# Two attention blocks in fp32: sums put between products, a bias made later, loads and statistics moved

## Chip, cores and metric

The kernel runs on one core of a Trainium2 chip. The metric is the device time of one execution in microseconds (us), lower is better. All data is fp32. The engines have short names: PE is the matrix engine (TensorE), DVE the vector engine (VectorE), ACT the scalar engine (ScalarE), POOL is GpSimd, and SP is SyncE, which here only issues transfers.

## What is computed

The input is x of shape (8, 512, 32, 32): eight samples of 512 channels at 1024 positions. Two attention blocks follow each other, each with a residual.

```python
# layer 0: group norm (32 groups), 8 heads of 64 channels
h = group_norm(x);  q, k, v = split(W_qkv h + b)
attn = softmax(q^T k / 8);  x = x + W_proj (v attn^T) + b_proj
# layer 1: one norm over the whole sample, one head of 512 channels
n = (x - mean) * rsqrt(var + eps)
q, k, v = Wq n + bq, Wk n + bk, Wv n + bv
attn = softmax(q^T k / sqrt(512));  x = x + Wo (v attn^T) + bo
```

## The kernel before

**Products.** Dense products are done by a seven-product scheme (Strassen's, in the form with sums S1 to S4 of one operand and T1 to T4 of the other), and many of those seven are split once more in the same manner. So most results are built from products into a bank of PSUM that DVE adds onto a tile in SBUF, or ACT copies there. The sums of operands (S, T) are made ahead by DVE or POOL.

**Order.** PE, ACT and DVE run in an order written out by hand (`tc.manual_schedule`); SP's and POOL's orders are set by a scheduler. Each phase is a Python generator that yields after each product or so, its *step*. `at_steps(steps, hooks)` runs the functions in `hooks[n]` after step n. Moving work to another hook thus moves it on its engine's queue. Each engine takes its queue in order.

**Samples.** For each sample b, `layer0` does the softmax attention of layer 0 in 64 *units* (a group of scores, its exponentials, its values), with extra work hung on units by `at_units`. `middle` then makes, for sample b + 1, layer 0's v, the first pair of q and k, and (after the projection of b) the second pair, "qk13"; `attention1` does layer 1 of sample b. For b = 0 to 6 layer 1's q is made by `make_q_twice`, for b = 7 by another path.

The steps and lines that the change touches (numbers are those of the kernel before):

- `make_twice` (in layer 0 of b = 0): for each part of a weight, `begin` re-loads its rows (L595, tile again_wqk), `sums` makes S1 to S4 on DVE (L520, tile wqk_twice), and the last one stores the result (L611). One of these steps is done every second unit. The same units hold `fold`, three transfers on SP (L1300 to L1302), and `folded`, a DVE sum (L1307), which `sum_couple` on PE (L1315, ps_sum) needs.
- qk13 in `middle`: 14 steps of products (L1027) with copies by ACT (L641), then six line products (L1034); between them DVE adds the tiles c12 and c22 (L664) and takes each line's bank (L661). `norm.moments` (L333) makes two passes of ACT over a 128x512 quarter of x for layer 1's statistics; there are eight of them.
- `make_q_twice` with `seven_by_two_steps`: groups z and w, then (second phase) groups c and d. c's products (L1697) go into tiles c by ACT (L703) or DVE (L705); d's are all added onto z (L705). Between the phases DVE puts the bias on z and w (L712). At the end `plus` on DVE adds half of c onto z (L710), for k = 1 and then 0, and POOL adds w to c (L735), which tells the last quarters of q. Here z, c and w carry names z_q, c_q and w_q.
- `norm.untaken` and `norm.bias` (L391 to L402): small DVE instructions on at most four columns. The result of `bias` is used at the end of layer 1 only.
- x_stat: for b + 2, x is loaded once more and ACT makes its moments (L333) during q's second phase and v.
- v of layer 1 (`make_v_twice`, `by_two_steps`): 14 steps of products (L1055), whose results ACT copies (L641) or DVE adds (L638), then six line steps (L783; A11, S2, S3, each for line 0 and line 1) that DVE takes into c_v (L659) after adding c12 and c22 (L664). A line's next product goes onto the same bank, so it waits for DVE's reading of the one before.
- in these v steps `finish_q(n)` (L1777, tile s_q) makes q's S1 to S4, two DVE instructions each, and `halve_a("S1")` (L520, tile S_twice) four more sums. POOL halves S4 and A22 (L520) afterwards, behind its small statistics (L350 to L356).

Of the kernel before, what the change touches and what calls it, by code (L numbers as in the profile page):

```python
# [65 lines left out]
def two_attention_blocks(  # L66
# [18 lines left out]
    nc = tc.nc  # L85
# [494 lines left out]
    def quarters_of_rows(a, rows_of):  # L580
        return {f"A{i + 1}{j + 1}": rows_of(i, a)[:, j, :] for i in range(2) for j in range(2)}

    def make_twice(name, ns=range(2), rows_of=None, engine=nc.vector):

        pairs, key = TWICE.get(name, PAIRS), f"{name}_twice"
        if key not in stored:
            stored[key] = dram.tile([P, len(pairs) * N], FP, tag=key, name=f"stored_{key}")

        def rows_again(n):
            parts, t = {}, tile2(f"again_{name}_{n}")
            for i, (a, _) in enumerate(pairs[n]):
                at = A_PARTS.index(a) * HALF
                nc.sync.dma_start(t[:, i, :], stored[name][:, at : at + HALF])  # L595
                parts[a] = t[:, i, :].rearrange("p (k o) -> p k o", k=2)
            return lambda i, a: parts[a][:, :, i * P : (i + 1) * P]

        def steps_of(n):
            made = []  # L600

            def begin():
                rows = rows_of or rows_again(n)
                made.extend([rows, flat(tile2(f"{name}_twice_{n}"))])

            def sums(i):
                rows, t = made
                sums_a(quarters_of_rows(pairs[n][i][0], rows), t[:, i * HALF : (i + 1) * HALF], engine)
                if i == len(pairs[n]) - 1:
                    size = len(pairs[n]) * HALF  # L610
                    nc.sync.dma_start(stored[key][:, n * N : n * N + size], t[:, :size])  # L611

            return [begin] + [lambda i=i: sums(i) for i in range(len(pairs[n]))]

        return [step for n in ns for step in steps_of(n)]

    def make_all(*args, **more):
        for step in make_twice(*args, **more):
# [60 lines left out]
    def seven_by_two_steps(multiply, at, z, c, w, bias, name):  # L679

        def group(tag, products, use_of):
            line, single = (banks(t, f"ps_{t}{tag}_{name}") for t in "so")
            spares.extend([single[:, 1, :], line[:, 1, :]])  # L690
            line, single = line[:, 0, :], single[:, 0, :]
            for bank, x, y, start, fresh, r, t in [
                (line, "A11", "B11", True, True, 0, 0), (single, "A12", "B21", True, False, 0, 0),
                (line, "S2", "T2", False, True, 0, 1), (single, "S1", "T1", True, True, 1, 1),
                (line, "S3", "T3", False, False, 1, 1), (single, "S4", "B22", False, False, 0, 1),
                (line, "A22", "T4", False, True, 1, 0),
            ]:
                multiply(bank, products, x, y, start)
                tiles, always = use_of
                to = at(tiles, r, t)  # L700
                of = bank[:, : len(products) * 2 * P].rearrange("p (i q) -> p i q", i=to.shape[1])
                if fresh and not always:
                    nc.scalar.copy(to, of)  # L703
                else:
                    nc.vector.tensor_tensor(to, of, to, ALU.add)  # L705
                yield

        def plus(to, x, y, by=None):
            if by is None:
                nc.vector.tensor_tensor(to, x, y, ALU.add)  # L710
            else:
                nc.vector.scalar_tensor_tensor(to, x, by, y, ALU.add, ALU.add)  # L712

        def in_order(order, **groups):
            for n in order:
                next(groups[n])
                yield

        spares.clear()
        first = dict(z=group("z", REST[0], (z, False)), w=group("w", REST[1], (w, False)))  # L720
        yield from in_order("zzwzwzwzwzwzww", **first)
        for k in range(2):
            plus(z[k][:, 1, :], z[k][:, 0, :], z[k][:, 1, :], bias and bias(k, 0))
        for k in range(2):
            plus(w[k], w[k], z[k][:, 1, :], bias and bias(k, 1))
        spares.clear()
        c_of, d_of = [("S1", "T1"), ("A22", "T4")], [("A12", "B21"), ("S4", "B22")]
        second = dict(c=group("c", c_of, (c, False)), d=group("d", d_of, (z, True)))
        yield from in_order("ccdcdcdcdcdcd", **second)
        next(second["d"])  # L730
        for k in [1, 0]:
            plus(z[k][:, 1, :], z[k][:, 1, :], c[k][:, 0, :])
        for k in range(2):
            both = w[k].unsqueeze(1).to_broadcast([P, 2, HALF])
            nc.gpsimd.tensor_tensor(c[k], c[k], both, ALU.add)  # L735
        yield
        spares.clear()

# [407 lines left out]
    def layer0(bs, qs, ks, vs, b, norm_next, ending, begun):  # L1146


        if b == 0:
            vs[:] = places_v(f"0_{b}")  # L1150
            hooks = {}
# [64 lines left out]
        if b == 0:  # L1216
            w = next_weight("qk13")
            w.finish()
            p0 = waiting[-1]

            def bias0():
                rows = Rows([(bias_0, p0.moving)], 1, "bias0", room("bias0"))
                rows.store()
                rows.fetch(nc.sync)
                throughs[:] = [rows]

            hooks = {
                4: [lambda: norm_next.mean_of_all()], 5: [lambda: norm_next.variance_of_all()],
                **{6 + half: [lambda half=half: norm_next.normed(norm_next.xs, [half])] for half in range(2)},
                8: [bias0, lambda: combine.first(norm_next.xs), lambda: score(0)],  # L1230
                9: [combine.second, lambda: score(1), lambda: make_all("qk13", rows_of=both_of(w))],
            }
            hooks[7].append(p0.finish)
            at_steps(together(*pairs_qk(w, 1, bs, qs, ks, b)), hooks)
            steps = []
            for name, ns in [("v0", range(2)), ("p0", range(2)), ("wqk1", range(4))]:
                of = [columns_of(of) for of in waiting if of.name == name]
                steps += make_twice(name, ns, of[0] if of else None)
            for n, step in enumerate(steps):
                at_units.setdefault(3 + 2 * n, []).append(step)  # L1240
        else:
            ps[0], = begun
            accs[units[0][:2]] = ps[0]
            score(1)
            if norm_next is not None:

                def load_next():
                    norm_next.xs = load_x(b + 1, nc.sync)

                at_units[8] = [load_next]  # L1250
                at_units[12] = [norm_next.of_deviation]
                for n in range(2 * NC):
                    at_units[14 + n] = [lambda cc=n % NC, half=n // NC: norm_next.normed_one(norm_next.xs, cc, half)]
                at_units[22] = [lambda: combine.take(norm_next.xs)]
                for n in range(4):
                    at_units[23 + 3 * n] = [lambda n=n: combine.make(n + 1)]
        for n, step in enumerate(ending):
            at_units.setdefault(n + 2, []).append(step)
        last = norm_next is None
# [129 lines left out]
        for i in range(2, len(units) + 2):  # L1389
# [10 lines left out]
            name = f"0_{b}_{pair}_{g}"  # L1400
# [36 lines left out]
        norm = norm1(xs, b)  # L1437
# [50 lines left out]
        hooks = {2: [ready.load]}  # L1488
# [7 lines left out]
    def middle(b, bs, twice_w, twice_b, comb, combine2, bias, hooks_v, divisions):  # L1496
# [15 lines left out]
        hooks = {n: [division] for n, division in enumerate(divisions)}  # L1512
# [16 lines left out]
        pairs = places_qk(1, b + 1)  # L1529
        hooks = {10: [ready.load]}  # L1530
        for n in range(2 * NC):
            hooks.setdefault([2, 4, 6, 8, 10, 12, 14, 14][n], []).append(
                lambda cc=n % NC, half=n // NC: norm.moments(cc, half, half == 0)
            )
        for n in range(1, 5):
# [29 lines left out]
    def attention1(xs, norm, ready, b, at_values, norms):  # L1565

        last = b + 1 == B
# [169 lines left out]
        else:  # L1737
            hooks = {
                0: [norm.both_halves], 6: [lambda: spares.insert(0, spares[3])], 7: [norm.mean_of_all],
                10: [lambda: spares.pop(0)], 11: [norm.deviation],  # L1740
                13: [norm.untaken, lambda: biases.append(norm.bias())],
                16: [lambda: twice_w.append(WeightTwice("wvo1"))],
            }
            if b + 2 < B:
                later = []
# [24 lines left out]
        def finish_q(n):  # L1770
            of[f"S{n}"] = halves(tile2(f"s{n}_q_{b}"))
            x, y, op = {
                1: ("A21", "A22", ALU.add), 2: ("S1", "A11", ALU.subtract),
                3: ("A11", "A21", ALU.subtract), 4: ("A12", "S2", ALU.subtract),
            }[n]
            for k in range(2):
                nc.vector.tensor_tensor(of[f"S{n}"][k], of[x][k], of[y][k], op)  # L1777

        v_pairs = places_v(f"1_{b}")
        for n in range(1, 5):  # L1780
            hooks_v.setdefault(2 * n + (3 if last else 5), []).append(lambda n=n: finish_q(n))
        hooks_v.setdefault(17 if last else 15, []).append(lambda: halve_a("S1"))
        at_steps(make_v_twice(w, twice_w[0], bs, twice_b, v_pairs, f"v_1_{b}"), hooks_v)


# [891 lines left out]
```

## Time and profile before

| | before |
|---|---|
| median of 3 runs | 2799.12 us (2797.68 to 2799.32) |
| profiled execution | 2798.8 us, its span 2797.1 us |
| granted clock of PE | 0.999 |
| PE busy | 2772.4 us, 99% of the span |
| DVE, ACT, POOL busy | 77%, 42%, 21% |
| DMA | 358.59 MB, mean 128 GB/s |

One stretch of b = 0, from the table of busy times by window:

| stretch, us | what runs | length | PE busy | DVE busy | ACT busy | POOL busy |
|---|---|---|---|---|---|---|
| 248.0 to 293.0 | q and k pair 0, projection | 45.00 | 45.00 | 35.89 | 6.17 | 15.77 |
| 293.0 to 316.2 | q and k pair 1 (qk13) | 23.20 | 22.47 | 16.35 | 15.82 | 21.49 |
| 316.2 to 338.4 | layer 1's q | 22.20 | 21.83 | 14.77 | 11.90 | 3.13 |
| 338.4 to 363.1 | layer 1's v | 24.70 | 23.33 | 19.04 | 11.55 | 14.03 |
| 363.1 to 453.0 | scores and values of layer 1 | 89.90 | 89.90 | 69.29 | 23.43 | 25.50 |

The span runs from the program's first to its last instruction; the time of an execution has 1.7 us around it. "Busy" is the time in which an engine has an instruction under way. PE's ends are modelled, and its short stops are partly hidden in the busy time. The list of waits says which engine's idle time ended with which release, as total, times and longest.

### The profile page before, as it was taken

To read this page: it belongs to the slowest core of one execution; us is meant where nothing else is said; L and a number is where in the kernel's file an instruction comes from. 1 tells how busy PE (TensorE), PEld (TensorE's weight loads), DVE (VectorE), ACT (ScalarE), POOL (GpSimd) and SP (SyncE) were. 2 spreads that over 40 slices of the span, in tenths; PEclk is the share of its full clock that TensorE was granted. 3 is DMA by queue.
4 is the path that set the end of the run, shared out by engine and by line. 5 is a ranking of instruction groups with operands and counts; after the bars stand their busy time and mean duration, and the time that the engine had idled before them with its cause. 6 is when DMAs were issued, how large, how long until landed. Compare 5 with 4: busy or idle time off the path is not lost.

```text
span 2797.1 us, 41715 instructions
## 1 busy us (share of the span) xinstructions
PE 2772.4 (99%) x16318; PEld 1645.5 (59%) x16318; DVE 2147.5 (77%) x3023; ACT 1186.7 (42%) x1911; POOL 598.2 (21%) x612
## 2 busy tenths in 40 slices
PE   9999999999999999999999999999999999999999
PEld 5437764377643776447764477645676356753375
DVE  6787677876778777887778776877768877688877
ACT  3462533625346153462535524255342643226621
POOL 0001440014400253003530044300432005320121
PEclk9999999999999999999999999999999999999999
DMA  7545514265142642326432263322633236141101
GB/s 256 204 129 196 202 57 140 58 210 182 57 140 58 211 181 74 126 62 230 155 115 86 77 226 143 127 81 70 240 128 140 69 102 238 69 169 31 35 16 39
DMA packets 114525, 358.59 MB, mean 128 GB/s; under 512 B 25052, under 2 KB 25852, under 8 KB 107920
## 3 DMA queue, kind: packets, MB, share of 16 engines
q1 hardware_dynamic: 89856, 299.68, 31.3%
q10 hardware_dynamic: 24464, 56.16, 6.1%
q8 instruction: 130, 2.13, 0.3%
q14 instruction: 75, 0.61, 0.1%
HBM read 252.77 MB, written 79.21 MB: 119 GB/s over the span
## 4 chain that ended last, share of the span: by engine, by line
PE 91%; DVE 5%; POOL 1%; issue 1%; ACT 1%; DMA 1%; ACTq 0%; SPq 0%; DVEq 0%; POOLq 0%
PE ps_o L1185 15%; PE s L1136 15%; PE ps_o L1995 10%; PE ps_l L1827 5%; PE ps_l_qk L1034 5%; PE ps_s L1810 4%; PE ps_l_v L783 4%; PE ps_s L1827 4%; PE ps_s_qk L1027 3%; PE ps_l_p L768 3%; PE ps_o_qk L1027 2%; PE ps_s_v L1055 2%; PE ps_s_p L1092 2%; PE ps_s_two L2125 2%; PE ps_o_v L1055 2%; PE ps_o_two L2125 1%
## 5 line engine op out<-in xcount | busy, mean ns | idle before, releaser
L940 ACT ACTIVATE p<-s 128x1024 f32<-128x1024 f32 x505 | 516.3, 1024 | 308.5 <-PE s L1136 301.4
L942 DVE TENSOR_TENSOR acc<-acc,p 128x1024 f32<-128x1024 f32 x384 | 468.7, 1221 | 61.8 <-ACT p L940 52.6
L1136 PE MATMUL s<-qk_back,qk_back 64*64 64x512 f32 x3528 | 457.4, 590 | 0.0
L1185 PE MATMUL ps_o<-p,v_back 64*64 64x512 f32 x3528 | 455.3, 589 | 0.0
L1185 PEld LDWEIGHTS ps_o<-p,v_back 64*64 64x64 f32 x3528 | 134.8, 133 | 243.7 <-issue 239.9
L1136 PEld LDWEIGHTS s<-qk_back,qk_back 64*64 64x64 f32 x3528 | 132.5, 133 | 245.6 <-issue 216.2
L537 POOL TENSOR_TENSOR B_twice_p<-o 128x512 f32<-128x512 f32 x14 | 20.9, 1493 | 1067.9 <-DVE o L1205 1067.9
L1995 PE MATMUL ps_o<-t_p,s_v 128*128 128x512 f32 x384 | 169.6, 596 | 0.0
L1801 ACT ACTIVATE p<-p,factor 128x512 f32<-128x512 f32 (+1 forms) x112 | 84.5, 780 | 113.3 <-DVE p L1837 86.4
L1815 ACT COPY p<-ps_s 128x512 f32<-128x512 f32 x96 | 53.1, 588 | 175.9 <-PE ps_s L1810 175.9
L1837 DVE TENSOR_TENSOR p<-ps_l,p 128x512 f32<-128x512 f32 x136 | 91.6, 688 | 44.8 <-PE ps_l L1827 43.2
L1995 PEld LDWEIGHTS ps_o<-t_p,s_v 128*128 128x128 f32 x384 | 71.8, 190 | 88.4 <-issue 88.0
L659 DVE TENSOR_TENSOR c_v<-ps_l_v,c_v 128x512 f32<-128x512 f32 x120 | 79.2, 686 | 44.8 <-PE ps_l_v L783 44.7
L537 POOL TENSOR_TENSOR B_twice<-x 128x512 f32<-128x512 f32 x23 | 35.6, 1550 | 358.6 <-DVE x L1447 177.2
L942 DVE TENSOR_TENSOR acc<-p,p 128x1024 f32<-128x1024 f32 x57 | 69.7, 1222 | 49.1 <-ACT p L940 49.1
L1034 PE MATMUL ps_l_qk<-t,w_qk 128*128 128x512 f32 x224 | 100.3, 595 | 2.3 <-DVE c_k L661 2.1
L1837 DVE TENSOR_TENSOR p<-ps_s,p 128x512 f32<-128x512 f32 x112 | 74.8, 686 | 31.3 <-PE ps_s L1827 29.7
L641 ACT COPY c_q<-ps_s_qk 128x512 f32<-128x512 f32 x56 | 32.6, 583 | 139.4 <-PE ps_s_qk L1027 139.4
L641 ACT COPY c_v<-ps_s_v 128x512 f32<-128x512 f32 x90 | 52.7, 585 | 91.1 <-PE ps_s_v L1055 91.1
L1798 POOL TENSOR_TENSOR acc<-acc,p 128x512 f32<-128x512 f32 x48 | 83.5, 1740 | 13.3 <-ACT p L1801 10.8
L1034 PEld LDWEIGHTS ps_l_qk<-t,w_qk 128*128 128x128 f32 x224 | 42.0, 190 | 58.3 <-issue 50.2
L373 POOL TENSOR_TENSOR rstd<-rstd,minus_half 128x4 f32<-128x4 f32 (+1 forms) x16 | 12.9, 806 | 273.1 <-DVE rstd L372 273.1
(693 smaller groups left out, 5815.4 us busy)
## 6 DMA issues: line engine op xcount, KB each, us to landing
x<-in_x SPq DMA_DIRECT2D x64, 512.0 KB, 9.3
qk_back<-kept_qk SPq DMA_DIRECT2D x56, 512.0 KB, 6.6
w_qk<-stored_qk SPq DMA_DIRECT2D x14, 1792.0 KB
fold<-acc SPq DMA_DIRECT2D x56, 256.0 KB, 2.9
qk_twice<-stored_qk_twice ACTq DMA_DIRECT2D x28, 512.0 KB, 4.8
kept_v<-c_v SPq DMA_DIRECT2D x28, 512.0 KB, 4.4
kept_qk<-c_q SPq DMA_DIRECT2D x28, 512.0 KB, 2.6
kept_qk<-c_k SPq DMA_DIRECT2D x28, 512.0 KB, 3.5
```

The costliest lines, as they stand in the source:

```text
L783: nc.tensor.matmul(bank[:, u * 2 * P : (u + 1) * 2 * P], bs[b][:, k, n * P : (n + 1) * P], w[a][:, k, :], start=fresh and u == k == 0, sto ...
L940: nc.scalar.activation(p, s, AF.Exp, scale=factor)
L942: nc.vector.tensor_tensor(acc, first, p, ALU.add)
L1027: nc.tensor.matmul(bank[:, i * 2 * P : (i + 1) * 2 * P], parts[a][x], twice_b[v][y], start=start and i == 0, stop=True, skip_group_check=True,
L1034: nc.tensor.matmul(bank, of(i, a)[:, k, :], bs[v][:, k, :], start=start and k == 0, stop=k == 1, skip_group_check=True,)
L1055: nc.tensor.matmul(bank[:, (2 * i + u) * P : (2 * i + u + 1) * P], twice_b[v][y][:, u * P : (u + 1) * P], parts[a][x], start=start and i = ...
L1136: nc.tensor.matmul(s[cols, j, :], ks[pair][k0 // HALF][rows, k0 % HALF : k0 % HALF + HD], qs[pair][g][rows, :], start=True, stop=True,)
L1185: nc.tensor.matmul(o[cols, half, :], vs[n][kt % 4 // 2][rows, h, c0 : c0 + HD], p[rows, j, :], start=kt == 0, stop=kt == NT - 1,)
L1810: nc.tensor.matmul(bank, bs[v][:, k, t * P : (t + 1) * P], of[a][k], start=a == "A11" and k == 0, stop=k == 1, skip_group_check=True,)
L1827: nc.tensor.matmul(bank[:, u * 2 * P : (u + 1) * 2 * P], v[y][:, u * P : (u + 1) * P], a[x], start=start and u == 0, stop=True, skip_group ...
L1837: nc.vector.tensor_tensor(at(r, t), bank, at(r, t), ALU.add)
L1995: nc.tensor.matmul(bank, v_parts[kt // 2][a][:, kt % 2, c * P : (c + 1) * P], p_parts[kt // 2][b][:, kt % 2, cols], start=fresh and kt == ...
```

## The change

- `make_twice` gets an argument `early`, set for weights that have to be re-loaded (wqk1): the re-load for the next part then stands in front of the sums of the present one.
- In `seven_by_two_steps` the additions of c onto z, and POOL's of w to c, become `exchange(k)`: k = 0 between d's fifth and sixth product, k = 1 after the seventh. Before, both stood after the seventh, k = 1 first for z.
- In qk13 the moments of step 12 are moved to step 14.
- In layer 1's q for b < 7, `norm.bias` moves from step 13 to step 20.
- In layer 1's v for b < 7, `finish_q(1..4)` move from steps 7, 9, 11, 13 to 5, 7, 9, 11, and `halve_a("S1")` from step 15 to 13.

The order of PE's instructions stays as it was, as does POOL's but for its two additions of w to c; on ACT one copy of c_k changes places with two passes.

```diff
--- before.py
+++ after.py
@@ -580,7 +580,7 @@
     def quarters_of_rows(a, rows_of):
         return {f"A{i + 1}{j + 1}": rows_of(i, a)[:, j, :] for i in range(2) for j in range(2)}
 
-    def make_twice(name, ns=range(2), rows_of=None, engine=nc.vector):
+    def make_twice(name, ns=range(2), rows_of=None, engine=nc.vector, early=False):
 
 
 
@@ -612,7 +612,13 @@
 
             return [begin] + [lambda i=i: sums(i) for i in range(len(pairs[n]))]
 
-        return [step for n in ns for step in steps_of(n)]
+        steps = [steps_of(n) for n in ns]
+        if early:
+            begins = [of.pop(0) for of in steps]
+            for of, begin in zip(steps, begins[1:]):
+                of.insert(0, begin)
+            steps[0].insert(0, begins[0])
+        return [step for of in steps for step in of]
 
     def make_all(*args, **more):
         for step in make_twice(*args, **more):
@@ -726,13 +732,17 @@
         spares.clear()
         c_of, d_of = [("S1", "T1"), ("A22", "T4")], [("A12", "B21"), ("S4", "B22")]
         second = dict(c=group("c", c_of, (c, False)), d=group("d", d_of, (z, True)))
-        yield from in_order("ccdcdcdcdcdcd", **second)
-        next(second["d"])
-        for k in [1, 0]:
+
+        def exchange(k):
             plus(z[k][:, 1, :], z[k][:, 1, :], c[k][:, 0, :])
-        for k in range(2):
             both = w[k].unsqueeze(1).to_broadcast([P, 2, HALF])
             nc.gpsimd.tensor_tensor(c[k], c[k], both, ALU.add)
+
+        yield from in_order("ccdcdcdcdcdc", **second)
+        exchange(0)
+        yield from in_order("d", **second)
+        next(second["d"])
+        exchange(1)
         yield
         spares.clear()
 
@@ -1235,7 +1245,7 @@
             steps = []
             for name, ns in [("v0", range(2)), ("p0", range(2)), ("wqk1", range(4))]:
                 of = [columns_of(of) for of in waiting if of.name == name]
-                steps += make_twice(name, ns, of[0] if of else None)
+                steps += make_twice(name, ns, of[0] if of else None, early=not of)
             for n, step in enumerate(steps):
                 at_units.setdefault(3 + 2 * n, []).append(step)
         else:
@@ -1529,7 +1539,7 @@
         pairs = places_qk(1, b + 1)
         hooks = {10: [ready.load]}
         for n in range(2 * NC):
-            hooks.setdefault([2, 4, 6, 8, 10, 12, 14, 14][n], []).append(
+            hooks.setdefault([2, 4, 6, 8, 10, 14, 14, 14][n], []).append(
                 lambda cc=n % NC, half=n // NC: norm.moments(cc, half, half == 0)
             )
         for n in range(1, 5):
@@ -1738,8 +1748,8 @@
             hooks = {
                 0: [norm.both_halves], 6: [lambda: spares.insert(0, spares[3])], 7: [norm.mean_of_all],
                 10: [lambda: spares.pop(0)], 11: [norm.deviation],
-                13: [norm.untaken, lambda: biases.append(norm.bias())],
-                16: [lambda: twice_w.append(WeightTwice("wvo1"))],
+                13: [norm.untaken], 16: [lambda: twice_w.append(WeightTwice("wvo1"))],
+                20: [lambda: biases.append(norm.bias())],
             }
             if b + 2 < B:
                 later = []
@@ -1778,8 +1788,8 @@
 
         v_pairs = places_v(f"1_{b}")
         for n in range(1, 5):
-            hooks_v.setdefault(2 * n + (3 if last else 5), []).append(lambda n=n: finish_q(n))
-        hooks_v.setdefault(17 if last else 15, []).append(lambda: halve_a("S1"))
+            hooks_v.setdefault(2 * n + 3, []).append(lambda n=n: finish_q(n))
+        hooks_v.setdefault(17 if last else 13, []).append(lambda: halve_a("S1"))
         at_steps(make_v_twice(w, twice_w[0], bs, twice_b, v_pairs, f"v_1_{b}"), hooks_v)
 
 
```

## Prediction

> **What bounds the kernel now.** TensorE (PE) does. Part 1 of the page, the busy table, gives it 99% of the span, and the chain of waits gives it 91% of the path. So only time in which PE stands still can be won, and no edit takes matmuls away.
>
> ```profile
> PE 2772.4 (99%) x16318; PEld 1645.5 (59%) x16318; DVE 2147.5 (77%) x3023; ACT 1186.7 (42%) x1911; POOL 598.2 (21%) x612
> ...
> PE 91%; DVE 5%; POOL 1%; issue 1%; ACT 1%; DMA 1%; ACTq 0%; SPq 0%; DVEq 0%; POOLq 0%
> ```
>
> The busy table hides part of each stop, because a matmul's end is modelled. I therefore read the list of waits first (total, times, longest), to find where PE waits for another engine, and then took start-to-start times from the timeline.
>
> ```profile
> DVE s_q L1777 <- POOL c_q L735: 15.2, 7, 2.2
> ...
> PEld ps_l_v L783 <- DVE c_v L659: 13.6, 14, 1.8
> ...
> PEld ps_l_qk L1034 <- DVE c_k L661: 8.1, 7, 2.2
> ...
> PEld ps_sum L1315 <- DVE acc L1307: 7.1, 7, 2.3
> ...
> PEld ps_oc_q L1697 <- DVE c_q L705: 5.4, 7, 0.8
> ...
> DVE wqk_twice L520 <- DMA again_wqk<-stored_wqk: 4.8, 2, 2.7
> ```
>
> Seven times almost always means once in each of the seven samples whose layer 1 makes q in two phases (b = 0 to 6). The timeline of b = 0 (start, duration, engine, line; idle before it and its releaser in brackets) shows each stop:
>
> ```profile
> 177.85 1.06 PE L1315 MATMUL ps_sum<-acc,ones 64*32 64x512 f32 x8 [1.37 <-DVE acc L1307]
> ...
> 308.32 0.56 ACT L641 COPY c_k<-ps_s_qk 128x512 f32<-128x512 f32 x1
> ...
> 310.91 5.42 PE L1034 MATMUL ps_l_qk<-t,w_qk 128*128 128x512 f32 x12 [0.73 <-DVE c_k L661]
> ...
> 327.06 0.16 DVE L402 TENSOR_TENSOR bias<-v_b,bias 128x4 f32<-128x4 f32 x1
> ...
> 329.79 0.68 DVE L705 TENSOR_TENSOR c_q<-ps_oc_q,c_q 128x512 f32<-128x512 f32 x1
> ...
> 330.53 1.13 PE L1697 MATMUL ps_oc_q<-T_twice,wqk_twice 128*128 128x256 f32 x4 [0.37 <-DVE c_q L705]
> ...
> 345.27 1.29 DVE L1777 TENSOR_TENSOR s_q<-z_q,c_q 128x512 f32<-128x512 f32 x2 [2.18 <-POOL c_q L735]
> ...
> 353.77 0.68 DVE L659 TENSOR_TENSOR c_v<-ps_l_v,c_v 128x512 f32<-128x512 f32 x1
> ...
> 354.52 3.71 PE L783 MATMUL ps_l_v<-w_wvo,t 128*128 128x256 f32 x16
> ...
> 358.00 0.94 DVE L520 TENSOR_TENSOR S_twice<-s_q,S_twice 128x256 f32<-128x256 f32 x1
> ...
> 359.60 3.72 PE L783 MATMUL ps_l_v<-w_wvo,t 128*128 128x256 f32 x16 [1.37 <-DVE c_v L659]
> ```
>
> A 128x256 matmul starts every 0.215 us, a 128x512 one every 0.43. The 16 that start at 354.52 should be followed at 357.97, and are at 359.60: 1.64 us lost, a slow restart of 0.10 included. Counted so over the trace, these stops cost:
>
> - v's lines (L783): 1.64 in b = 0 to 5, 1.38 in b = 6; 11.2 in all.
> - q and k of layer 0, pair 1 (L1034): 1.00 in b = 0, 1.67 in b = 4, 0.31 in the others; 4.2.
> - q's second phase (L1697): 0.64 in each, and in b = 1 a further 1.2; 5.7.
> - the sum in layer 0 of b = 0 (L1315): 1.95, once.
>
> Together 23.0 us, 0.8% of the span: the most that the edits can bring.
>
> [...] S_twice (L520) takes 0.78 to 0.94 us beside POOL at 355 to 359, the same shape (spare, L520) 0.42 alone at 369, and sums from PSUM (L705) stay at 0.69 beside POOL at 341. [...] the three instructions of V's bias, on 1 to 4 columns, take 0.15, 0.23 and 0.16. [...]
>
> **The change, part by part.** The instructions are the same in number and kind, and PE's and POOL's orders are unchanged but for POOL's two additions of w to c, now c[0] first.
>
> *Weights of layer 0, b = 0.* The re-load of each part of wqk1 is put one step, two units of 1.72 us, ahead of its use; SP issues two of its loads ahead of a fold's three. DVE's wait of 2.67 at 171.84 goes, so the fold's sum (L1307, 176.58 to 177.80) comes some 2.7 earlier and PE no longer loses 1.95. The other samples, with no such loads, have no stop there. Gain 1.95 (bounds -2 to 1.95: on SP the fold's three transfers now stand behind the second early load, and if that waits for a free buffer, the fold is late and PE's stop as long as now or twice that).
>
> *The moments moved from step 12 to 14.* ACT, in order, does c_k's copy at 306.38, then two passes (1.94), then c_k's other copy at 308.32, for which DVE and then PE wait. Now the copies are adjacent: the second ends near 307.5, DVE adds the two c_k tiles (0.7, or 1.28 with POOL) and takes the bank from 308.5 to 309.25, before PE's 310.03. The passes end when they did. Gain 4.2 (3 to 4.2).
>
> *V's bias moved to step 20.* Three instructions, 0.52 from 326.62 to 327.14, leave the DVE chain in front of L712 and L705, so PE's next start moves from 330.53 to 330.02. At step 20 DVE stands idle for 0.51 (until ACT's c_q at 333.76): free. But ACT is late next. It starts its passes over x_stat at 329.59, when a load lands, and its copies of c follow behind them, at 331.21 and 333.17; PE must wait for each before it rewrites the bank. In b = 0 the second allows PE's bank at 333.78 instead of 334.09. Doing this sum with each sample's copies leaves 0.22, 0, 0.10, 0.60, 0, 0.21 and 0.60 (b = 6 has no x_stat): 1.7. If the loads land earlier, up to 4.5; if later, 0.
>
> *Additions of C into Z, and the finishing of q.* The first addition goes into DVE's idle 1.03 ahead of 337.75. POOL's first addition can then start near 337.4 rather than 340.17, and the pair (2 x 2.54) ends near 343.4, allowing 0.7 for the second DVE addition[...], instead of 345.24. So finish_q's first sum, two steps earlier, starts at 343.0 to 343.5, and two of its eight instructions more fit before DVE's c_v at 346.86, which waits for ACT. From c_v's second (347.75, set by PE) DVE runs without a gap, a sum every 0.60: 6 to the end of finish_q and c_v, then halve_a's four (0.37 each alone), then c12 and the line's addition. The old order had eight before c12. So the addition starts at 347.75 + 0.61 + 6 x 0.60 + 1.47 + 0.60 = 354.03, and PE may go on at 354.78, when it is due at 354.51: 0.27 lost, 0.37 with the restart. The stop of 1.64 is gone since the four are now in front. Gain 1.27, but POOL's small statistics lie beside the four here; I take 1.15, in six samples 6.9. In b = 6 there are no statistics, and POOL's halving of S4 begins just when DVE's four do: they take 2.93, as at 2411.55, and c12 0.5 more, so the stop grows from 1.38 to some 2.2: minus 0.8. Sum 6.1; bounds -4 (all samples as b = 6, and some more) to 9.
>
> Sum: 1.95 + 4.2 + 1.7 + 6.1 = 13.95, some 14.0. The profiled execution took 2798.8 (span 2797.1, 1.7 around it); less 14.0 is 2784.8. The median of the runs is 0.3 above it: **2785.1**.
>
> **The rivals.**
>
> 1. *The four in front are a new wait.* If halve_a meets POOL in every sample, v's gain is -0.8 x 7 = -5.6 to 0, and the sum 2.3 to 7.9: 2791 to 2797. For it: 0.94 against 0.42 in b = 6. Against: in b = 0 to 5, POOL's S4 waits for statistics that ACT ends at 353.3, and starts at 355.34. Chance 0.12.
> 2. *PE loses nothing more.* The x_stat loads land early and the lines wait for nothing: 2777 to 2780. Against: ACT's copies have 0 to 0.6 us of room. Chance 0.13.
> 3. *Slower: finish_q waits on DVE's queue behind POOL.* Its first two sums (four instructions, 2.4) and one c_v (0.6) come before the c_v that PE allows at 347.75, so all behind is late by POOL's end less 344.75. If POOL gains no head start[...], POOL ends near 346.1 and everything is 1.35 late; with the halving under POOL as well (2.0 more) v's stop is 0.37 + 1.35 + 2.0 = 3.7. The loss is 7 x (3.7 - 1.6) = 14.7 against 7.85 from the other edits: 2806. It is slower by over 0.2% from a stop of 3.5, thus from POOL's end at 345.9, where 345.24 is now. Against: POOL's start moves up by 2.8. Chance 0.04.
> 4. *It does not do what it says*: the stops go but PE waits as long for the next engine. Some 2793.5 to 2799; chance 0.05.
>
> **How the numbers follow.** The forecast has 0.66 and a range of its own of 2781 to 2789, which takes in the bounds of the two smaller open costs (1.7, and 6.1 give or take 3). 0.2% is 5.6 us, about what a measurement of this kernel can tell from no change. Faster by more than that: the forecast, rival 2 and most of rival 1, 0.89. Within: 0.07. Slower: 0.04. The range to hold 8 in 10 takes the forecast with half of rivals 1 and 2: 2778.5 to 2791.
>
> **What would show it.** In the profile after, "PEld ps_l_qk <- DVE c_k" and "DVE wqk_twice <- DMA" should be gone; ps_oc_q's wait for DVE under 1 us in all, with waits for ACT's c_q copies in its place; ps_l_v still waiting for DVE, at S2 of line 0, about 0.3 us in b = 0 to 5 and 1.7 or more in b = 6; POOL's first c_q sum starting some 1.0 us before PE's first v product, where it starts 1.8 after it now. A v stop over 1.5 us in b = 0 to 5, or DVE waiting for POOL's c_q as long as now, would prove the largest term wrong.

## The result, and the profile after

The changed kernel takes 2782.11 us (median of 4 runs, 2781.19 to 2782.54); the kernel before, beside it, 2798.44 (4 runs). The ratio is 0.9941, with a 95% interval of 0.9924 to 0.9958: faster by 16.3 us, 0.6%. The forecast was 2785.1 in a range of 2778.5 to 2791.0. The profiled execution took 2782.46, with a span of 2780.7 (before: 2798.8 and 2797.1), again at a granted TensorE clock of 0.999.

The page of the kernel after, busy table and chain of waits:

```profile
PE 2770.3 (100%) x16318; PEld 1646.2 (59%) x16318; DVE 2139.4 (77%) x3023; ACT 1187.9 (43%) x1911; POOL 590.3 (21%) x612
...
PE 95%; DVE 2%; DMA 1%; ACT 1%; issue 0%; ACTq 0%; SPq 0%; DVEq 0%
```

PE has the same 16318 matmuls and fills the span; its share of the path rose from 91% to 95%, and DVE's fell from 5% to 2%. The list of waits of the kernel after (who waits, for whom: total us, times, longest) shows what replaced the stops:

```profile
PEld ps_l_v L793 <- DVE c_v L665: 5.4, 7, 2.5
...
PEld ps_sc_q L1707 <- ACT c_q L709: 2.7, 4, 1.0
...
PEld ps_oc_q L1707 <- ACT c_q L709: 1.7, 6, 0.3
PEld ps_oc_q L1707 <- DVE c_q L711: 1.7, 7, 0.2
...
PEld ps_l_qk L1044 <- DVE c_k L667: 0.8, 1, 0.8
```

v's wait fell from 13.6 to 5.4, of which 2.5 is one sample; qk's from 8.1 to 0.8; q's for DVE from 5.4 to 1.7, and waits for ACT's copies (2.7 and 1.7) came in its place. DVE's 15.2 for POOL's c_q and its 4.8 for the re-loaded weights are no longer there. The timeline of b = 0 shows v's part (after, lines of DVE, POOL and PEld in order of start):

```profile
334.56 2.36 POOL L739 TENSOR_TENSOR c_q<-c_q,w_q 128x1024 f32<-128x1024 f32 x1 [11.64 <-DVE z_q L716]
337.55 2.36 POOL L739 TENSOR_TENSOR c_q<-c_q,w_q 128x1024 f32<-128x1024 f32 x1 [0.63 <-DVE z_q L716]
340.13 1.28 DVE L1787 TENSOR_TENSOR s_q<-z_q,c_q 128x512 f32<-128x512 f32 x2
...
349.07 0.42 DVE L520 TENSOR_TENSOR S_twice<-s_q 128x256 f32<-128x256 f32 x1
...
350.20 0.42 DVE L520 TENSOR_TENSOR S_twice<-s_q,S_twice 128x256 f32<-128x256 f32 x1
350.54 0.69 DVE L670 TENSOR_TENSOR c_v<-c_v,c_v 128x512 f32<-128x512 f32 x1
351.14 0.68 DVE L665 TENSOR_TENSOR c_v<-ps_l_v,c_v 128x512 f32<-128x512 f32 x1
...
351.88 0.73 PEld L793 LDWEIGHTS ps_l_v<-w_wvo,t 128*128 128x128 f32 x4 [0.48 <-DVE c_v L665]
```

POOL ends its pair at 339.91, before DVE's s_q at 340.13 wants it, and the four halvings run alone at 0.42 us each. PE's next bank starts at 351.88, where 348.18 (start of the 16 matmuls before) plus 3.45 gives 351.64: 0.24 lost. In b = 6 the same code meets POOL:

```profile
2393.52 0.94 DVE L520 TENSOR_TENSOR S_twice<-s_q 128x256 f32<-128x256 f32 x1
...
2394.14 0.91 POOL L520 TENSOR_TENSOR S_twice<-S_twice,s_q 128x256 f32<-128x256 f32 x1
2394.39 0.94 DVE L520 TENSOR_TENSOR S_twice<-s_q,S_twice 128x256 f32<-128x256 f32 x1
...
2395.25 1.20 DVE L670 TENSOR_TENSOR c_v<-c_v,c_v 128x512 f32<-128x512 f32 x1
...
2397.11 5.04 PEld L793 LDWEIGHTS ps_l_v<-w_wvo,t 128*128 128x128 f32 x24 [2.49 <-DVE c_v L665]
```

A halving lasts up to 0.94 in place of 0.42, c12's sum (L670) 1.20 in place of 0.69, and PE stops for 2.25. One kernel thus shows the same DVE instructions with POOL's halving beside them (b = 6, POOL's L520 from 2392.54 on) and without it (b = 0, where POOL's begins at 352.44, behind them).

**A count without thresholds.** PE's order is the same in all these kernels, so each stage can be timed from the start of its first matmul to the start of the next stage's. The table gives, for each kernel, its stage lengths less those of the kernel before, summed over the samples, in us. "Start" is all before the first scores of b = 0 (106.2 us in the kernel before), with the first loads of the weights; in e3 to e5, whose edits lie behind it, it is 0.49 and 0.68 shorter and 0.17 longer. "To q" runs in b = 0 from these scores to the start of layer 1's q, and in the later samples from the end of v to the next q (the stops of ps_sum and ps_l_qk lie there). "All" ends at PE's last matmul.

| kernel | start | to q | q | v | all |
|---|---|---|---|---|---|
| changed | +0.40 | -6.01 | -1.81 | -7.24 | -14.65 |
| e1, re-load alone | -0.48 | -3.15 | -0.67 | 0.01 | -4.26 |
| e2, moments alone | -0.26 | -3.84 | -1.13 | -0.03 | -5.24 |
| e3, bias alone | -0.49 | 0.04 | -2.31 | -0.01 | -2.78 |
| e4, exchange alone | -0.68 | 0.07 | -0.66 | -0.02 | -1.30 |
| e5, finishing and halving alone | +0.17 | -0.36 | +1.74 | -3.48 | -1.91 |
| e6, changed, halving at 15 | +0.34 | -5.54 | -2.20 | -3.32 | -10.73 |
| e7, changed, passes later | +0.56 | -6.05 | -0.88 | -7.49 | -13.86 |
| e8, e6 and e7 | +0.36 | -6.05 | -0.89 | -3.66 | -10.24 |
| e9, changed, halving at 17 | +0.41 | -5.99 | -1.68 | -11.74 | -18.97 |
| e10, changed, passes spread | +0.14 | -5.96 | -4.94 | -7.32 | -18.05 |
| e11, e9 and e10 | +0.15 | -6.07 | -4.94 | -11.74 | -22.60 |
| e12, before, passes spread | -0.23 | 0.16 | -1.19 | -1.05 | -2.30 |

A *late load* means here that x_stat lands late, so that ACT's passes over it, and the copy of c_q behind them, are late and PE waits. The kernel before had one in b = 1 in its profiled execution, worth 0.9 to 1.2. So e1, e2 and e4, whose edits don't touch PE's waits for ACT in q, show that "gain" in q too (in e1 and e4 a late load in b = 0 takes 0.3 and 0.6 of it back), and so does e12. Of the span's 16.3 us, 14.65 are PE's; 1.7 lie between PE's last start and the end of the span, 7.27 before and 5.58 after. DVE's last sum ends 5.9 and 4.2 before the end, and after it only the final write is left. In the profiles of the seven kernels with the change (after, e6 to e11) this tail is 5.58 to 5.79; in the seven without it, it is 5.94 to 6.00 (e4, e5, e12) or 7.25 to 7.44 (before, e1 to e3). So most of the 1.7 varies without the change, and why the tail is shorter in all seven kernels with it was not traced: whether the change has a part in it stays open.

### The profile page after: what moved, and what is told of

Read it like the earlier page. It is cut to its first block, busy times and chain, and to the rows that moved or that the text cites. A ratio compares the mean times of both kernels' runs of the same rounds, so it can differ in the third digit from the quotient of the medians.

```text
span 2780.7 us, 41752 instructions
## 1 busy us (share of the span) xinstructions
PE 2770.3 (100%) x16318; PEld 1646.2 (59%) x16318; DVE 2139.4 (77%) x3023; ACT 1187.9 (43%) x1911; POOL 590.3 (21%) x612
## 4 chain that ended last, share of the span: by engine, by line
PE 95%; DVE 2%; DMA 1%; ACT 1%; issue 0%; ACTq 0%; SPq 0%; DVEq 0%
PE ps_o L1195 16%; PE s L1146 16%; PE ps_o L2005 10%; PE ps_l_qk L1044 5%; PE ps_l L1837 5%; PE ps_l_v L793 5%; PE ps_s L1820 4%; PE ps_s L1837 4%; PE ps_s_qk L1037 3%; PE ps_s_v L1065 3%; PE ps_o_qk L1037 3%; PE ps_l_p L778 3%; PE ps_o_v L1065 2%; PE ps_s_two L2135 2%; PE ps_s_p L1102 2%; PE ps_o_two L2135 1%
## 5 line engine op out<-in xcount | busy, mean ns | idle before, releaser
L667 DVE SCALAR_TENSOR_TENSOR c_q<-ps_l_qk,vec,c_q 128x512 f32<-128x512 f32 x56 | 40.8, 749 | 39.7 <-PE ps_l_qk L1044 39.7
```

## The experiments

In the edits shown below, lines are shortened (`...` for what is left out), and the `.append(...)` behind each `setdefault` is left out.

**e1 to e4: one edit at a time, on the kernel before.**

```diff
e1  -        return [step for n in ns for step in steps_of(n)]
    +        steps = [steps_of(n) for n in ns]
    +        if early:
...
    +                steps += make_twice(name, ns, of[0] if of else None, early=not of)
e2  -  [2, 4, 6, 8, 10, 12, 14, 14][n]
    +  [2, 4, 6, 8, 10, 14, 14, 14][n]
e3  -  13: [norm.untaken, lambda: biases.append(norm.bias())],
    +  13: [norm.untaken], ... 20: [lambda: biases.append(norm.bias())],
e4  +  exchange(k), as in the change, nothing else
```

> The kernel before with one edit alone: the re-load of each part of layer 0's weights in b = 0 one step earlier. Theory (four separate stops of TensorE, each taken away by its own edit): the stop in front of ps_sum in b = 0 goes, and s<-q,k of b = 0 starts some 2.0 us earlier (176.9 for 178.9); every later stage keeps its distance, so the span is 2.0 shorter, 2795. Rival (the stop goes but TensorE waits for the next fold or for the weights instead): 0 to 1 us, with a new wait of ps_sum or of s. Rival (SP's queue late): a longer wait of acc for kept parts, 0 to 2 us slower.

Measured: 2794.95 us, before 2797.96, ratio 0.9988 (0.9981 to 0.9995). Timeline of b = 0, e1; all 16 matmuls of ps_sum now run in one piece, where before (in the prediction's lines) the second eight waited:

```profile
174.95 0.18 PEld L1321 LDWEIGHTS ps_sum<-acc,ones 64*32 64x32 f32 x16 [0.81 <-DVE acc L1313]
174.95 1.09 PE L1321 MATMUL ps_sum<-acc,ones 64*32 64x512 f32 x16
```

The scores behind ps_sum in b = 0 start 2.4 us earlier, counted from the first scores of b = 0, and 0.7 of the stop of ps_l_qk in b = 0 goes as well: 3.1, more than expected. The 0.7 comes from two places that the edit doesn't touch: ACT's gap at its loads of wqk_twice is 1.02 where it was 1.31, and DVE's sum into c_k takes 0.87 where it took 1.28. Why the two changed with the shift in time was not traced.

> The kernel before with one edit alone: the moments of layer 0 measured after step 14 instead of step 12. Theory (separate stops): the stops of ps_l_qk go, 0.3 in five samples, 1.0 in b = 0 and 1.4 in b = 4, as they did with all edits together: 3.9 us, 2794 to 2795. Rival (they go only because other edits move the loads of the statistics in time): under 2 us. The wait of ps_l_qk for c_k should be gone from the list but for one.

Measured: 2794.77, ratio 0.9989 (0.9982 to 0.9996). "To q" falls by 3.84, as expected; ACT's two copies of c_k lie together and PE goes on without a wait in six samples. In b = 4, where the stop was 1.67, 0.3 of it stays. Timeline of b = 0 in e2:

```profile
304.65 3.60 PE L1034 MATMUL ps_l_qk<-x,w_qk 128*128 128x512 f32 x8
306.16 1.05 ACT L641 COPY c_k<-ps_s_qk 128x512 f32<-128x512 f32 x2
308.09 4.45 PE L1034 MATMUL ps_l_qk<-t,w_qk 128*128 128x512 f32 x10
```

> The kernel before with one edit alone: V's bias made after step 20 of q instead of step 13. Theory (separate stops, ScalarE's passes late next): ps_oc_q starts 0.53 us earlier in each of seven samples, and 0 to 0.8 of it is given back in front of ps_sc_q and ps_oc_q, where they wait for ScalarE's copies behind its passes over x_stat; 1.7 to 2.1 us in all, 2796 to 2797. Rival (the copies are late only because all else is earlier): the full 3.5 to 5.

Measured: 2797.03, ratio 0.9995 (0.9986 to 1.0004), which alone tells nothing from no change. In the trace ps_oc_q starts 0.53 us earlier in all seven samples, 3.7 in sum, and waits for ACT's copies take part of it back, in front of ps_sc_q (0.78 late in b = 0) and ps_oc_q: q is 2.31 shorter, of which 0.85 is the late load of b = 1. Timeline of b = 0, e3:

```profile
329.56 1.13 PE L1697 MATMUL ps_oc_q<-T_twice,wqk_twice 128*128 128x256 f32 x4
...
331.52 0.59 ACT L703 COPY c_q<-ps_sc_q 128x512 f32<-128x512 f32 x1
...
332.16 1.13 PE L1697 MATMUL ps_sc_q<-T_twice,wqk_twice 128*128 128x256 f32 x4 [0.61 <-ACT c_q L703]
```

The theory holds, with a gain that depends on when a load lands.

> The kernel before with one edit alone: the additions of C into Z, and GpSimd's two additions after them, put between the last products of q; the finishing of q and the halving of S1 stay where they were. Theory (an order on VectorE's queue, not GpSimd, sets v's stop): VectorE's wait for GpSimd's c_q (15.2 us in the list) goes, and yet v's stops stay at 1.6 us in b = 0 to 5, since the same ten additions and c_v's lie between TensorE's last bank of ps_s_v and its first line: 0 us gained, within 1 us of the kernel before. Rival (VectorE's idle 2.2 us behind GpSimd is what v waits for): the stop falls by more than 1 us per sample, 7 to 9 us gained.

Measured: 2796.68, ratio 0.9996 (0.9987 to 1.0005). v is unchanged to 0.02 us in every sample. DVE's wait for POOL is gone, and DVE stands about as long further on (timeline of b = 0, e4):

```profile
342.97 1.28 DVE L1780 TENSOR_TENSOR s_q<-z_q,c_q 128x512 f32<-128x512 f32 x2
346.81 0.69 DVE L638 TENSOR_TENSOR c_v<-ps_s_v,c_v 128x512 f32<-128x512 f32 x1 [2.56 <-ACT c_v L641]
```

So the wait that heads the prediction's list, 15.2 us, was worth nothing alone: behind it the next instruction of DVE waits for ACT. The rival, 7 to 9 us gained, is out.

**e5: the finishing of q and the halving, without the exchange.**

```diff
-  hooks_v.setdefault(2 * n + (3 if last else 5), [])
-  hooks_v.setdefault(17 if last else 15, [])    # halve_a
+  hooks_v.setdefault(2 * n + 3, [])
+  hooks_v.setdefault(17 if last else 13, [])
```

> The kernel before with the finishing of q two steps earlier and the halving of S1 at step 13 instead of 15, but with the additions of C into Z and GpSimd's two additions left where they were. Theory (the exchange gains nothing alone but is what lets the earlier finishing run): VectorE still waits for GpSimd until 345.2 of b = 0 and two additions more now stand in front of c_v, so everything from c_v on is 0.5 us later than with all edits; v's stop is 0.75 to 0.9 in b = 0 to 5, for 1.64 before and 0.35 with all edits, and some 2.8 in b = 6: 6 x 0.8 - 1.4 = 3 us gained in all (2 to 5). Rival (the exchange isn't needed): the stop is 0.35 as with all edits, 6.7 gained. Rival (c_v's banks, late behind the two additions, stop TensorE at ps_s_v too): 0 gained or slower.

Measured: 2795.30, before 2798.14, ratio 0.9988 (0.9982 to 0.9995). v: -0.82 in b = 0 to 5, +1.47 in b = 6, sum -3.48, expected 3. Timeline of b = 0, e5:

```profile
347.20 1.30 DVE L1777 TENSOR_TENSOR s_q<-z_q,c_q 128x512 f32<-128x512 f32 x2 [2.18 <-POOL c_q L735]
...
353.00 3.62 PE L783 MATMUL ps_l_v<-w_wvo,x 128*128 128x256 f32 x16
...
357.22 0.94 PEld L783 LDWEIGHTS ps_l_v<-w_wvo,t 128*128 128x128 f32 x5 [1.01 <-DVE c_v L659]
```

DVE still stands 2.18 us for POOL, now ahead of more work, and PE's line starts 0.77 late (357.22 less 353.00 and 3.45). In v the exchange alone gives 0, this part alone 3.5, both 7.2: the exchange frees time that only the earlier finishing uses. (q was 1.71 longer in b = 0 here, a late load.)

**e6 to e8: what is left, first attempts, on the changed kernel.**

```diff
e6  -  hooks_v.setdefault(17 if last else 13, [])
    +  hooks_v.setdefault(17 if last else 15, [])
e7  -  hooks.setdefault([14, 17, 19, 21][n], [])      # measure_later
    +  hooks.setdefault([19, 19, 21, 21][n], [])
e8  both
```

> The changed kernel with one thing put back: the halving of S1 at step 15 of v, behind the lines' first two additions, instead of 13. Theory (the earlier finishing and GpSimd's head start are what won, the halving in front is a cost): without its four instructions (1.5 us alone, some 3 beside GpSimd) in front, c12 and the line's first addition come 1.5 earlier and wait for TensorE instead; v's stops of 0.35 in b = 0 to 5 go, and the 2.35 of b = 6 falls to 0.8 or less: 3 to 4 us below the changed kernel, some 2778.5. Rival (the halving ahead of the lines is what took the stop away): v's stops come back to 1.4 to 1.6 in every sample, 7 us above the changed kernel.

Measured: 2786.42, before 2798.14, ratio 0.9958 (0.9944 to 0.9972): 4.3 above the changed kernel's median, where the theory said 3 to 4 below. The stops in front of the second bank went, 0.24 and 2.25, but another came at the third bank (timeline of b = 0, e6):

```profile
352.14 1.59 POOL L520 TENSOR_TENSOR S_twice<-s_q 128x256 f32<-128x256 f32 x2
352.69 0.45 DVE L520 TENSOR_TENSOR S_twice<-s_q 128x256 f32<-128x256 f32 x1
...
354.80 0.94 DVE L520 TENSOR_TENSOR S_twice<-s_q,S_twice 128x256 f32<-128x256 f32 x1
...
355.66 1.28 DVE L665 TENSOR_TENSOR c_v<-ps_l_v,c_v 128x512 f32<-128x512 f32 x2
...
356.40 0.92 PE L793 MATMUL ps_l_v<-w_wvo,t 128*128 128x256 f32 x3 [0.90 <-DVE c_v L665]
```

The halving beside POOL lasts from 352.69 to 355.66 and the addition that frees the bank stands behind it: 1.06 us. So the theory fell, and the changed kernel's place ahead of POOL is part of its gain in b = 0 to 5.

> The changed kernel with ScalarE's first two passes over x_stat put after step 19 of q instead of 14 and 17, that is behind its copies of c from ps_sc_q and ps_oc_q. Theory (what is left of q's stops is ScalarE waiting for a load with those copies behind it): the copies run at 13.2 and 15.0 us after q's start, TensorE's stops in front of ps_sc_q and ps_oc_q (3.8 us in all) go, and the passes end where the next copy is due: 3 to 4 us below the changed kernel. Rival (VectorE's additions from the same banks are what TensorE waits for): the stops stay, 0 to 1 us. Rival (the passes crowd into v's copies instead): the stops go and v's or the next ones grow by as much.

Measured: 2783.55, ratio 0.9949 (0.9936 to 0.9963): no gain, nearest to the last of the rivals. The stops for ACT in front of ps_sc_q and ps_oc_q went, and one of 0.68 came in front of ps_s_v in six samples (timeline of b = 0, e7), where PE waits for ACT's last copy of c_q, late behind four passes (a pass is here the mean and the square of one quarter, 1.6 us):

```profile
335.10 0.56 ACT L709 COPY c_q<-ps_sc_q 128x512 f32<-128x512 f32 x1
335.72 0.52 PEld L1065 LDWEIGHTS ps_s_v<-w_wvo,x 128*128 128x128 f32 x4 [0.92 <-ACT c_q L709]
```

> The changed kernel with both: the halving of S1 at step 15 of v, and the passes over x_stat behind q's copies. Theory: the two are separate stops, so their gains add: 6.5 to 7.8 us below the changed kernel, 2774 to 2776. Rival (one of the two is given back at the other): the better of the two alone, 2778 to 2779.

Measured: 2786.82, ratio 0.9960 (0.9946 to 0.9973); both losses are there side by side, "q" as in e7 and "v" as in e6.

**e9 to e12: what the misses taught.**

```diff
e9   +  hooks_v.setdefault(17, [])                     # halve_a
e10  +  hooks.setdefault([19, 19, 21, 25][n], [])      # measure_later
e11  both
e12  the kernel before with e10's line alone
```

> The changed kernel with the halving of S1 after step 17 of v in every sample, behind the additions of the lines' second banks, instead of 13. Theory (what counts is only which additions of a line, whose bank TensorE takes again, stand behind the halving): at 13 it delays the first line's additions by 0.24 (b = 6: 2.25), at 15 the second's by 1.30; at 17 only the third's stand behind it, and TensorE doesn't take those banks again until the scores. Both stops go: 6 x 0.35 + 2.3 = 4.4 us below the changed kernel, some 2778. Rival (the third additions, 1.3 to 2 us late, or the halvings behind them stop the scores instead): 0 to 1 us a sample given back, 0 to 3 below. Rival (there must be a stop wherever it is put): 4 above, as at 15.

Measured: 2777.26, before 2797.33, ratio 0.9929 (0.9916 to 0.9943). v is 11.74 shorter than before, 4.5 more than in the changed kernel, as expected (4.4). The halving still meets POOL, but nothing that PE needs stands behind it (timeline of b = 0, e9):

```profile
351.55 7.07 PE L793 MATMUL ps_l_v<-w_wvo,t 128*128 128x256 f32 x32
...
356.28 0.83 DVE L520 TENSOR_TENSOR S_twice<-S_twice,s_q 128x256 f32<-128x256 f32 x1
357.03 0.94 DVE L520 TENSOR_TENSOR S_twice<-s_q 128x256 f32<-128x256 f32 x1
```

The 32 matmuls of both banks run in one piece, to 358.45, when the scores start.

> The changed kernel with ScalarE's passes over x_stat after steps 19, 19, 21 and 25 of q instead of 14, 17, 19 and 21: three between the copies of c after steps 19 and 25, the fourth behind the last copy. Theory (four passes of 1.6 us are one too many for the 5 us between these copies, which is why moving them all gave back 0.68 a sample in front of ps_s_v): the last copy runs at 333.5 of b = 0 instead of 335.1 and neither ps_sc_q, ps_oc_q nor ps_s_v waits; 3.5 to 4 us below the changed kernel, some 2778.5. Rival (the fourth pass then delays v's first copies): the stop comes back at v's products, 0 to 2 below.

Measured: 2779.71, ratio 0.9939 (0.9926 to 0.9953). q is 4.94 shorter than before, 3.1 more than in the changed kernel; its stops for ACT are gone, and ps_s_v doesn't wait. ACT, in b = 0 of e10:

```profile
333.00 0.19 ACT L333 ACTIVATION_READ_ACCUMULATOR square<-x_stat,stat 128x1 f32 x1
333.10 0.59 ACT L709 COPY c_q<-ps_sc_q 128x512 f32<-128x512 f32 x1
333.58 0.63 ACT L333 ACTIVATE mean<-x_stat 128x512 f32<-128x512 f32 x1
```

Three passes end at 333.19, the copy stands right behind them, and the fourth is done at 335.16, before v's first copy at 335.71.

> The changed kernel with both: the halving of S1 after step 17 of v, and the passes over x_stat after steps 19, 19, 21 and 25 of q. Theory: separate stops, so the gains add, 7.5 to 8.4 us below the changed kernel, 2774 to 2775, ratio to the kernel before 0.9915. Rival (one is given back at the other): the better of the two alone, 2778.

Measured: 2774.94, ratio 0.9921 (0.9908 to 0.9935): 22.4 us below before and 7.2 below the changed kernel's median; PE's last start is 7.95 earlier than in the changed kernel, 0.25 of it the start. The gains add. The page of e11:

```profile
PE 2766.3 (100%) x16318; PEld 1647.8 (59%) x16318; DVE 2144.1 (77%) x3023; ACT 1188.0 (43%) x1911; POOL 587.7 (21%) x612
...
PE 99%; DVE 0%; issue 0%; POOL 0%; POOLq 0%
```

The chain of waits is now 99% PE.

> The kernel before with only the passes over x_stat moved to after steps 19, 19, 21 and 25 of q; V's bias stays at step 13. Theory (two stops in a row, of which the bias is the first and the passes are the second): the 0.53 of the bias in front of ps_oc_q stays in seven samples, and only what the passes cost goes: 0.9 to 1.3 us gained. Rival (the passes were the limit all along and the bias move was not needed): 3.5 us or more gained, with ps_oc_q starting 0.5 earlier.

Measured: 2794.98, ratio 0.9992 (0.9983 to 1.0000). In q only the late load of b = 1 goes; the other six samples stay within 0.02 us. So the bias was the first stop and the passes are the second, and moving the second alone gains only where a load was late (1.19, expected 0.9 to 1.3). Unexpected: v shrank by 0.21 in five samples, where the first halving now ran before POOL's (0.42 for 0.78).

## Why the prediction was right

The waits that it named are those that the runs show, and the sum lies near, but partly because errors cancel. The forecast was 14.0 us; PE gained 14.65, and 15.05 without the slower start. By its steps:

- **Re-load of weights.** Foreseen 1.95. The stop went and gave 2.4, and 0.7 more went with it at ps_l_qk (e1). The bound below zero did not come about: ps_sum waits 0.81 in e1, as in a sample without re-loads (before: 7.1 over seven samples, 2.3 of it in b = 0, so 0.8 in each of the others).
- **Moments.** Foreseen 4.2, 3.84 alone (e2). Not all of ps_l_qk's waits went, as foreseen: in b = 4 one of 0.8 in the list is left, which costs PE 0.3. The two edits share 0.66 in b = 0 (3.10 and 0.96 alone, 3.40 together), so together they gave 6.01, where the sum had 6.15: the errors nearly cancel.
- **Bias.** Foreseen 1.7, measured 1.81, in the way foreseen: ps_oc_q earlier by 0.53, then ACT's copies behind x_stat's passes. That the numbers lie so near is luck. By sample they don't: foreseen 0.22, 0, 0.10, 0.60, 0, 0.21, 0.60; measured -0.11, 0.93, 0.49, 0.03, 0.50, -0.57, 0.54. The passes start 13.1 to 14.2 us after q's start in the six samples, from the load's landing, and in other executions of the same order the sample that suffers is another (before: b = 1, by 0.9 to 1.2; e5, with q's order as before: b = 0, by 1.71). The step that failed is reading each sample's landing time as its own: the six samples without b = 1 gave 0.88 where 1.73 was foreseen, and b = 1's late load in the trace of before, foreseen to stay, gave the other 0.93. That ps_oc_q would wait under 1 us for DVE was wrong too: it is 1.7.
- **Additions and finishing.** Foreseen 6.1, measured 7.24. POOL starts 0.96 before v's first product (foreseen 1.0). The 0.7 allowed for DVE's second addition, between POOL's two, was an estimate of mine: POOL stands 0.63 there, and the addition takes 0.95 (336.52 to 337.47). The halving runs alone in b = 0 to 5 and meets POOL in b = 6, with a stop of 2.25, or 2.35 with the slow restart, which the foreseen 2.2 has in it. The term mis-sized is b = 0 to 5: I took 1.15 for each, having taken 0.12 off for POOL's small statistics beside the halving. They lay beside it in b = 0 (349.67 to 352.4) and cost DVE nothing, 0.42 a halving (POOL's L351 took 0.78, where it took 0.21 before): 1.34 to 1.39 was gained. Another 0.08 a sample was in the count of the stop, 1.64, where e9, without a stop there, is 1.72 shorter.
- **Interplay.** The prediction costed the exchange and the finishing as one step. e4 (0) and e5 (-3.48) bear that out: the two alone don't add up to the 7.24.
- **Rivals.** The halving as a new wait in every sample (rival 1) came in b = 6 alone, and in all samples only with the halving at step 15, at another bank (e6). Rival 2, nothing more lost, is e11, which needed two more moves; its 22.60 is close to the 23.0 that the prediction counted as the most. Rival 3's place, DVE held behind POOL, exists without the exchange (e5), where the stop is 0.77, 0.87 with the restart, in b = 0 to 5, and is not slower; POOL's end at 346.1, from which rival 3 has its loss, was an estimate of mine. The stops moved to the next engine (rival 4) only in q: of the 3.7 that ps_oc_q's earlier start is worth, waits for ACT's copies took 3.1 (q of e10 less q of the changed kernel).
- **A wrong line.** The sums from PSUM that stay at 0.69 beside POOL are not those of L705, whose last ends at 339.30, before POOL's additions begin at 340.17, but L638's, at 341.51 and 342.41, 0.69 each while POOL's additions run (340.17 to 345.24).

The profile and the medians agree on 16.3 us, but 1.7 of the profile's is the tail behind PE, which the forecast did not speak of. Medians of before in later comparisons were 2797.3 to 2798.1, so 15.2 to 16.3 is what the runs support.

## What to carry to other kernels

A long wait in the list may be worth nothing: before moving work out of the way of a wait, look at what the waiting engine does next and whether that has another condition, because then only moving both pays (in v 0 and 3.5 alone, 7.2 together). When PE is full, ask of each late instruction which bank it stands in front of, and put optional work behind the last addition whose bank PE takes again soon: the same four instructions cost 0.24, 1.06 or nothing in b = 0 at three places two steps apart. Count the room between two fixed copies before moving passes into it: four passes of 1.6 us did not fit into 5, three did.

## What the hardware showed unexpectedly

- **A group of four matmuls whose weight load waited a little takes 0.10 us more, 0.97 for 0.87, though its first matmul starts on time.** In the changed kernel ps_oc_q starts at 327.01, on time, 0.87 after ps_od_q, and yet the next group starts at 327.98, not 327.87. The list has it as seven waits of 0.2 us for DVE's c_q (1.7 in all). It is left in e10 and e11 as well. Where the 0.10 is spent was not traced further. Timeline of b = 0, after:

```profile
326.14 1.03 PE L1707 MATMUL ps_od_q<-x,w_wqk 128*128 128x256 f32 x4
327.01 1.13 PE L1707 MATMUL ps_oc_q<-T_twice,wqk_twice 128*128 128x256 f32 x4
327.98 1.03 PE L1707 MATMUL ps_sd_q<-B_twice,wqk_twice 128*128 128x256 f32 x4
329.16 1.13 PE L1707 MATMUL ps_sc_q<-T_twice,wqk_twice 128*128 128x256 f32 x4 [0.16 <-ACT c_q L709]
```

- **The landing of the same load varies by some 1 us and more between samples and executions.** In the changed kernel x_stat's transfers take 9.7 to 12.0 us from issue to landing, and ACT's first pass starts 13.13 to 14.20 us after q's start in the six samples of one execution, and in b = 0 of e5 it starts 15.14 after, where the kernel before has 13.42 there: q is 1.71 longer. What delays a load was not traced. Edits worth 1 to 2 us in such a stage can't be judged from one profile by the stage's length alone.
